# A coupled-map automaton on TensorE: ring products in pairs on two row tiles, and the convolution map of the same image beside it

## The chip, the core and the metric

The kernel runs on one NeuronCore of a Trainium2 chip. The metric is the device time of one execution in microseconds, the median of three runs. A profile is one further execution, recorded by the hardware profiler.

In the profile PE is TensorE's matmul side, PEld its weight loads, DVE VectorE, ACT ScalarE, POOL GpSimd and SP SyncE. POOL and SP issue the DMAs here, each in the order of its own queue. L393 means line 393 of the kernel before.

## The reference

The input has 32 images of 8 channels and 256 x 256 pixels. Four layers follow one another, each on a group-normalized input with its result added to the input. The change is in the first layer only:

```python
drive = x[:, :C_OUT]
grid = drive
for _ in range(STEPS):                       # 15 steps
    mapped = R * grid * (1.0 - grid)
    local = _conv(mapped, K_local, groups=C_OUT)      # 3x3, one kernel per channel
    physics = (1.0 - EPS) * mapped + EPS * local
    grid = (1.0 - BETA) * physics + BETA * drive
cml_out = jnp.clip(grid, 0.0001, 1.0 - 0.0001)
h = jax.nn.relu(_conv(x, Wp, bp))            # 3x3, 8 -> 128
nca_out = jax.nn.sigmoid(_conv(h, Wu, bu))   # 1x1, 128 -> 8
gin = jnp.concatenate([x, cml_out, nca_out], axis=1)
g = jax.nn.sigmoid(_conv(jax.nn.relu(_conv(gin, Wg1, bg1)), Wg2, bg2))   # 3x3, 24 -> 8, then 1x1
return g * cml_out + (1.0 - g) * nca_out
```

Below, the 15 steps are the automaton (`lattice` in the code), `h` and `nca_out` the map, and the last lines the gate. The remaining layers are a quantized 3x3 convolution, a 3x3 convolution and a 5x5 box filter; they run after the first layer has finished for all images, in a second part of the kernel that the change leaves alone.

## The kernel before

All data is fp32. An fp32 product appears in the trace as two matmul instructions, each with its weight load.

**The automaton.** Six of the eight channels (`CP = 6`) are computed on TensorE, the other two on VectorE. For TensorE the image is cut into patches of 16 rows by 8 columns: the 128 pixels of a patch lie on the 128 partitions, and the 512 patches of a channel on the free dimension. Neighbours within the patch come from one product with a 128 x 128 matrix (`patch_sb`, L391). Neighbours in the surrounding patches come from a second product that is added to it (`ring_sb`, L393). Its input, the tile `rings`, holds 80 rows, copies of the border rows of the state, shifted to the neighbouring patch: 16 for the left column, 16 for the right, and 24 each for the rows above and below (8 pixels times the patch itself and its two side neighbours). `spread` makes these copies with four SP DMAs (L259), each row with the data of three channels.

The channels are in two halves of three (`HALF`). For each half in a step the code issues three patch products, three ring products, three vector operations that add the drive out of PSUM (L402), and, after some other work, three squarings on ScalarE that write the next state (L419), and `spread`. PSUM has three buffers for these products. The two remaining channels are nine multiply-adds on VectorE (`tap`, L338), three beside the first half and six beside the second, then a clamp and the next state (L412, L413); `edges` copies the border rows of their strips with two SP DMAs (L263, L264).

**Map and gate.** `gated` is a generator of small pieces of work for PE, ACT, DVE and POOL. An image has eight chunks (`NCH`) of 512 columns; a chunk has four batches of four products `ph` (L633), each followed by a relu to `hh` (L638) and then by products with 32 output columns into `pn` (L610), four of which go to different column tiles. Six DMAs per batch bring the inputs `im` from `xn_d` (L505), a DRAM copy of the normalized image with borders. `close` takes the sigmoid of `pn` into `nh`, a tile in SBUF with room for four chunks, and issues small copies of its border rows (L480). The gate of a chunk begins five batches after the chunk. It loads the quarter image `xq` from `nr_d` and the automaton's result `cq` from `cr_d`, multiplies them and `nh` (L531, L539, L543), applies a second product (L548), mixes the results in seven vector operations (L561 to L568) and stores to `x1_d` (L569).

**The order** is written out by hand in one pass. Each `yield` of `lattice` and of `gated` gives a planned duration. The main loop at the end steps through `lattice(b)` and, after each yield, takes pieces of `gated` until their planned times have used up those of the automaton. `place` holds the chunk that the map has reached. Map and gate of image b-1 are taken beside the automaton of image b; beside image 0 there is nothing. `errands(b)` issues the loads, stores and statistics around an image one at a time, one per half step, on POOL and VectorE: the store of the normalized image to `xn_d` (L273), the load of the next image, the store to `nr_d` (L296), and to `xr_d` (L311).

Of the kernel before, what the change touches and what calls it, by code (L numbers as in the profile page):

```python
# [9 lines left out]
F32 = mybir.dt.float32  # L10
# [7 lines left out]
P = 128  # L18
C = 8
# [20 lines left out]
    (32, 8, (RB - 1) * PW, 1, -1 - SY, 3, SY),  # L40
    (56, 8, 0, 1, 1 - SY, 3, SY),
)
RING = 80
# [3 lines left out]
HALF = CP // 2  # L47
RQ = 4
BLOCK = 6.3
# [17 lines left out]
def kernel(  # L67
# [100 lines left out]
    with ExitStack() as es:  # L168
# [9 lines left out]
        ring_sb = const(wt, ring, [RING, CP, P], "ring_sb")  # L178
# [41 lines left out]
        nh = wt.tile([P, 8, WP], F32, name="nh")  # L220
        zero = wt.tile([C, WP], F32, name="zero")
        states = [wt.tile([P, HALF, SN], F32, name=f"state{i}") for i in range(2)]
        rings = [wt.tile([RING, HALF, SN], F32, name=f"rings{i}") for i in range(2)]
# [4 lines left out]
        for t in (*xbs, nh, zero, strip):  # L228
            nc.gpsimd.memset(t, 0.0)
        for t in (*states, *rings):  # L230
            nc.gpsimd.memset(t, 0.25)
# [5 lines left out]
        nr_d = [dram.tile([P, HB, WP], F32, name=f"nr_d{i}") for i in range(3)]  # L237

        cr_d = [dram.tile([P, HB, WP], F32, name=f"cr_d{i}") for i in range(3)]
        for t in xn_d:  # L240
            nc.sync.dma_start(
                window(t, 0, [[HP * WP, C], [(HP - 1) * WP, 2], [1, WP]]),
                nh[0:C, 0:2, :],
            )

        def inner(c):

            return states[c // HALF][:, c % HALF, AT : AT + TX * SY].rearrange("p (x y) -> p x y", y=SY)[:, :, 0:TY]

        def spread(half):  # L250

            long = (HALF - 1) * SN + RN
            state = states[half]
            row = state.ap[0][0]
            to = rings[half].rearrange("p c n -> p (c n)")
            for q, n, p, step, far, m, by in RINGS:
                at = p * row + AT + far
                dims = [[step * row, n]] + ([[by, m]] if m > 1 else []) + [[1, long]]
                nc.sync.dma_start(to[q : q + n * m, 0:long], window(state, at, dims))  # L259
# [6 lines left out]
        def errands(b):  # L266
# [3 lines left out]
            if b >= 0:  # L270
                xb = xbs[b % 2]
                for r in four:
                    nc.gpsimd.dma_start(  # L273
                        window(
                            xn_d[b % 3], (1 + r.start) * WP,
                            [[HP * WP, C], [RB * WP, HB], [1, 4 * WP]],
                        ),
                        xb[:, r, :].rearrange("p r w -> p (r w)"),
                    )
                    yield  # L280
# [47 lines left out]
        def lattice(b, ahead):  # L328
# [21 lines left out]
            )  # L350
            yield 5
            for t4 in range(TX // 4):
# [6 lines left out]
                if t4 == 0:  # L359
                    nc.vector.tensor_scalar(  # L360
                        xi, xi, st[:, 0:1], st[:, 1:2], ALU.subtract, ALU.mult
                    )
                if t4 == 4 and b > 0:
                    store(b - 1)
                if t4 == 1:
# [7 lines left out]
            for c in range(CP):  # L373
# [6 lines left out]
                if c % HALF == HALF - 1:  # L380
                    spread(c // HALF)
                yield 1.5
            yield 4
            for step in range(STEPS):
                for half in range(2):
                    mine = range(HALF * half, HALF * half + HALF)
# [5 lines left out]
                    for c in mine:  # L392
                        nc.tensor.matmul(  # L393
                            pss[c % HALF], ring_sb[:, c, :],
                            rings[half][:, c % HALF, 0 : TX * SY].rearrange(
# [4 lines left out]
                    for c in mine:  # L400
                        ps = pss[c % HALF]
                        nc.vector.scalar_tensor_tensor(ps, ps, FLOOR, dr[:, c], ALU.max, ALU.add)  # L402
                    if step == STEPS - 1:
                        for c in mine:
                            nc.vector.tensor_scalar(
                                dr[:, c], pss[c % HALF], 0.0001, 1.0 - 0.0001, ALU.max, ALU.min
# [636 lines left out]
```

## Time and profile before

| what | us |
|---|---|
| median of three runs | 16303.53 |
| lowest and highest of the runs | 16277.27 and 16305.33 |
| the profiled execution | 16318.33 |
| span of its profile, first to last instruction | 16316.6 |
| automaton of image 0 begins | 33.8 |
| automaton of image 1 and map of image 0 begin | 381.7 |
| last automaton ends | 13342.8 |
| last store of the first layer (L569) | 13594.8 |

The first layer is 83% of the span. The page has 42888 matmul instructions in it, twice the number of fp32 products. Times in the profile's answers count from the start of the span. The page's share of busy PE must be read with care, since a matmul's end is modelled and matmuls overlap; starts are better evidence than durations. For the DMAs of SP the page gives no time to landing.

### The profile page before, as it was taken

How to read it: one execution, taken by the hardware profiler on the slowest of the kernel's cores; microseconds unless marked ns; L12 is line 12 of the kernel's file. 1: busy time of each engine (PE TensorE's matmuls, PEld its weight loads, DVE VectorE, ACT ScalarE, POOL GpSimd, SP SyncE). 2: the span in 40 equal slices, each digit the busy share in tenths (PEclk: the TensorE clock that was granted, in tenths of full speed). 3: DMA queues.
4: the chain of work that ended last, by engine and by line, in shares of the span. 5: the costliest groups of instructions: out<-in, count | busy, mean ns of one | idle time of the engine just before them, and what ended most of it. 6: DMA issues, size and time to landing. Idle time of an engine off the chain costs nothing.

```text
span 16316.6 us, 141125 instructions
## 1 busy us (share of the span) xinstructions
PE 15452.2 (95%) x42888; PEld 6215.7 (38%) x42888; DVE 11705.9 (72%) x14652; ACT 5726.7 (35%) x8862; POOL 5598.2 (34%) x9491
## 2 busy tenths in 40 slices
PE   6999999999999999999999999999999997999999
PEld 2333333333333333333333333333333332333333
DVE  7777777777777777777777777777777764555554
ACT  2433444443434434443434444343444442111110
POOL 1333333333333333333333333333333342111111
PEclk7999999999999999999999999999999998999999
DMA  4766666666666666666666666666666664555554
GB/s 104 148 146 144 150 147 144 147 150 146 149 144 148 150 147 147 144 147 145 147 142 149 148 144 147 141 148 146 147 149 147 146 134 98 119 119 119 119 118 105
DMA packets 1057742, 2276.12 MB, mean 139 GB/s; under 512 B 419740, under 2 KB 623508, under 8 KB 1050724
## 3 DMA queue, kind: packets, MB, share of 16 engines
q0 software_dynamic: 704512, 1492.80, 40.6%
q1 hardware_dynamic: 352484, 774.29, 23.4%
q8 instruction: 356, 5.83, 0.2%
q14 instruction: 390, 3.19, 0.1%
HBM read 1078.04 MB, written 471.38 MB: 95 GB/s over the span
## 4 chain that ended last, share of the span: by engine, by line
PE 74%; DVE 13%; DMA 7%; ACT 3%; issue 2%; SPq 1%; POOL 0%; DVEq 0%; ACTq 0%; POOLq 0%
PE ph L633 17%; PE psc L391 14%; PE psc L393 13%; PE pg L531 9%; DVE acc L338 7%; PE psv L725 5%; PE pn L610 5%; PE psv L811 4%; DMA qb<-qh 3%; DMA rings<-state 2%; PE psv L729 2%; PE pq L548 1%; PE pg L543 1%; PE pg L539 1%; DVE psc L402 1%
## 5 line engine op out<-in xcount | busy, mean ns | idle before, releaser
L338 DVE SCALAR_TENSOR_TENSOR acc<-strip,taps_sb,acc 128x1024 f32<-128x1024 f32 x3840 | 4930.4, 1284 | 124.8 <-DMA strip<-strip 4.7
L505 POOL DMA_DIRECT2D im<-xn_d x6144 | 3458.3, 566 | 3250.0 <-PE ph L633 1434.7
L633 PE MATMUL ph<-im,wp_sb 72*128 72x512 f32 x8192 | 4091.7, 615 | 308.8 <-ACT hh L638 251.3
L638 ACT ACTIVATE hh<-ph,bp_sb 128x512 f32<-128x512 f32 x4096 | 2755.8, 690 | 4441.9 <-PE ph L633 4385.7
L402 DVE SCALAR_TENSOR_TENSOR psc<-psc,flat 128x512 f32<-128x512 f32 x2880 | 1921.4, 696 | 2813.0 <-PE psc L393 2797.2
L391 PE MATMUL psc<-state,patch_sb 128*128 128x512 f32 x5760 | 2812.0, 626 | 74.1 <-ACT state L419 63.3
L393 PE MATMUL psc<-rings,ring_sb 80*128 80x512 f32 x5760 | 2713.5, 607 | 129.8 <-DMA rings<-state 129.8
L633 PEld LDWEIGHTS ph<-im,wp_sb 72*128 72x128 f32 x8192 | 1489.5, 193 | 2425.4 <-issue 1587.8
L419 ACT ACTIVATE state<-psc,minus 128x512 f32<-128x512 f32 x2688 | 1690.2, 690 | 1818.8 <-DVE psc L402 1713.1
L391 PEld LDWEIGHTS psc<-state,patch_sb 128*128 128x128 f32 x5760 | 1114.5, 199 | 1696.2 <-issue 1375.7
L393 PEld LDWEIGHTS psc<-rings,ring_sb 80*128 80x128 f32 x5760 | 1114.7, 194 | 1576.8 <-issue 1545.7
L569 POOL DMA_DIRECT2D x_d<-xc x256 | 146.9, 574 | 3493.1 <-DVE xc L564 3416.6
L811 PE MATMUL psv<-xr,w_sb 128*128 128x512 f32 x2560 | 1162.9, 600 | 1.3 <-DVE xr L792 1.3
L610 PE MATMUL pn<-hh,wu_sb 128*32 128x512 f32 x8192 | 1133.9, 609 | 3.3 <-ACT hh L638 3.3
L776 POOL DMA_DIRECT2D x_d<-x x512 | 321.0, 643 | 1941.0 <-DVE x L770 1696.3
L725 PE MATMUL psv<-xh,w_sb 128*128 128x512 f32 x1536 | 753.0, 629 | 9.6 <-issue 9.6
L531 PE MATMUL pg<-xq,wg_sb 128*128 128x512 f32 x1536 | 749.3, 626 | 0.0
L754 ACT ACTIVATE x<-psv,b_sb,sc 128x512 f32<-128x512 f32 x256 | 199.3, 779 | 1466.2 <-PE psv L729 1465.8
L531 PE MATMUL pg<-cq,wg_sb 128*128 128x512 f32 x1536 | 713.7, 601 | 0.0
L811 PEld LDWEIGHTS psv<-xr,w_sb 128*128 128x128 f32 x2560 | 466.1, 189 | 610.8 <-issue 606.0
L338 DVE SCALAR_TENSOR_TENSOR acc<-strip,taps_sb,d 128x1024 f32<-128x1024 f32 x480 | 613.2, 1277 | 0.0
L831 DVE TENSOR_TENSOR y<-psv,y 128x512 f32<-128x512 f32 x256 | 177.1, 692 | 593.7 <-PE psv L811 593.7
(163 smaller groups left out, 12188.9 us busy)
## 6 DMA issues: line engine op xcount, KB each, us to landing
im<-xn_d POOLq DMA_DIRECT2D x6144, 96.6 KB, 6.6
rings<-state SPq DMA_DIRECT2D x1920, 159.5 KB
rings<-state SPq DMA_DIRECT2D x1920, 106.3 KB
strip<-strip SPq DMA_DIRECT2D x960, 126.0 KB
xn_d<-xb POOLq DMA_DIRECT2D x128, 516.0 KB, 7.7
nr_d<-xb POOLq DMA_DIRECT2D x128, 516.0 KB, 7.2
xq<-nr_d POOLq DMA_DIRECT2D x128, 516.0 KB, 5.1
cq<-cr_d POOLq DMA_DIRECT2D x128, 516.0 KB, 7.9
```

The source lines that it names most:

```text
L338: nc.vector.scalar_tensor_tensor(acc, strip[:, dy : dy + RQ, dx : dx + W], taps_sb[:, 3 * dy + dx : 3 * dy + dx + 1], d2 if dy == 1 and dx ...
L391: nc.tensor.matmul(pss[-1], patch_sb[:, c, :], inner(c), start=True, stop=False)
L393: nc.tensor.matmul(pss[c % HALF], ring_sb[:, c, :], rings[half][:, c % HALF, 0 : TX * SY].rearrange("p (x y) -> p x y", y=SY)[:, :, 0:TY], ...
L402: nc.vector.scalar_tensor_tensor(ps, ps, FLOOR, dr[:, c], ALU.max, ALU.add)
L419: nc.scalar.activation(inner(c), pss[c % HALF], AF.Square, bias=minus)
L505: nc.gpsimd.dma_start(im[24 * dy : 24 * dy + 24, k, 0:run], window(xn_d[b % 3], at, [[HP * WP, C], [1, 3], [1, run]]),)
L531: nc.tensor.matmul(o, wg1_sb[:, s, dx, :], src[:, :, dx : dx + W], start=s == dx == 0, stop=False,)
L610: nc.tensor.matmul(pn[32 * q : 32 * q + 32, :], wu_sb[:, i, :], hh, start=i == 0, stop=i == 3,)
L633: nc.tensor.matmul(ph.rearrange("p (k w) -> p k w", w=W), wp_sb, im[:, :, j * WP : j * WP + W], start=True, stop=True,)
L638: nc.scalar.activation(hh, ph, AF.Relu, bias=bp_sb)
L725: nc.tensor.matmul(o, w[:, dx, :], src[:, 2 * i : 2 * i + 2, dx : dx + W], start=dx == 0, stop=False,)
L811: nc.tensor.matmul(pss[k].rearrange("p (c w) -> p c w", w=W), w3_sb[:, dx, :], xr[:, k, mine, dx : dx + W], start=dx == 0, stop=stop,)
```

## The change

**Ring products in pairs.** The channels are taken in pairs (0, 3), (1, 4), (2, 5). The ring has 56 rows rather than 80: the rows above and below are split into 8 for the patch itself and 4 for the two corners (2 pixels times two side neighbours). One channel of the pair has its rows at partitions 0 to 55 (`LOW`), the other at 64 to 119 (`HIGH`) of the same tile, so that the two ring products use the upper and the lower half of the array and write different PSUM buffers. The state is kept in two sets, one with pairs 0 and 1, one with pair 2 (`SETS`). `spread(i)` copies a whole set: six DMAs for each side, twelve together, each row with two channels for set 0 and one for set 1.

**Order within a step.** Three pairs follow each other with 0.8 + 0.8 planned us between them and 8.6 + 0.8 after the third, the same 12.6 per step as the two halves had. `spread` follows the squares of pair 1 and pair 2, and `edges` the latter. The nine multiply-adds are spread 2, 2 and 5.

**Map beside the same image.** The store to `xn_d` moves from `errands` to the head of `lattice`, right after the normalization, which moves up too. `place[1]` is a limit: beside image 0 the map may reach chunk 7 of that image; beside image b it finishes chunk 7 of image b-1 first and then, once `store(b-1)` is issued, goes up to chunk 7 of image b.

**The map's result in DRAM.** The gate starts 33 batches after its chunk, instead of 5. So `nh` goes to DRAM (`nh_d`, three buffers) by one store per chunk, `keep_result`, and the gate loads it back like the other two inputs (`nq`), with its border rows. The copies of border rows from SBUF go.

```diff
-    (32, 8, (RB - 1) * PW, 1, -1 - SY, 3, SY),
-    (56, 8, 0, 1, 1 - SY, 3, SY),
+    (32, 8, (RB - 1) * PW, 1, -1, 1, 0),
+    (40, 8, 0, 1, 1, 1, 0),
+    (48, 2, (RB - 1) * PW, PW - 1, -1 - SY, 2, 2 * SY),
+    (52, 2, 0, PW - 1, 1 - SY, 2, 2 * SY),
 )
-RING = 80
+RING = 56
+LOW, HIGH = 0, 64
-HALF = CP // 2
+PAIRS = CP // 2
+SETS = ((0, 2), (2, 1))
-BLOCK = 6.3
+BLOCK = 12.6
...
-        def spread(half):
-
-            long = (HALF - 1) * SN + RN
-            state = states[half]
-            row = state.ap[0][0]
-            to = rings[half].rearrange("p c n -> p (c n)")
-            for q, n, p, step, far, m, by in RINGS:
-                at = p * row + AT + far
-                dims = [[step * row, n]] + ([[by, m]] if m > 1 else []) + [[1, long]]
-                nc.sync.dma_start(to[q : q + n * m, 0:long], window(state, at, dims))
+        def spread(i):
+
+            long = (SETS[i][1] - 1) * SN + RN
+            to = rings[i].rearrange("p c n -> p (c n)")
+            for state, base in zip(states[i], (LOW, HIGH)):
+                row = state.ap[0][0]
+                for q, n, p, step, far, m, by in RINGS:
+                    at = p * row + AT + far
+                    dims = [[step * row, n]] + ([[by, m]] if m > 1 else []) + [[1, long]]
+                    nc.sync.dma_start(
+                        to[base + q : base + q + n * m, 0:long], window(state, at, dims)
+                    )
...
+            nc.vector.tensor_scalar(xi, xi, st[:, 0:1], st[:, 1:2], ALU.subtract, ALU.mult)
+            for r in range(0, RB, 4):
+                nc.gpsimd.dma_start(
+                    window(
+                        xn_d[b % 3], (1 + r) * WP, [[HP * WP, C], [RB * WP, HB], [1, 4 * WP]]
+                    ),
+                    xb[:, r : r + 4, :].rearrange("p r w -> p (r w)"),
+                )
...
                 if t4 == 4 and b > 0:
                     store(b - 1)
+                    place[1] = NCH * (b + 1) - 1 if b + 1 < B else NCH * B
...
-            for c in range(CP):
+            for c in (0, 3, 1, 4, 2, 5):
...
-                if c % HALF == HALF - 1:
-                    spread(c // HALF)
+                if c >= PAIRS + 1:
+                    spread(c - PAIRS - 1)
...
+            taps_of = (((1, 0), (1, 1)), ((1, 2), (0, 0)), ((0, 1), (0, 2), (2, 0), (2, 1), (2, 2)))
             for step in range(STEPS):
-                for half in range(2):
-                    mine = range(HALF * half, HALF * half + HALF)
+                for j in range(PAIRS):
+                    i = j // 2
+                    mine = (j, PAIRS + j)
...
-                    for c in mine:
+                    for ps, base in zip(pss, (LOW, HIGH)):
                         nc.tensor.matmul(
-                            pss[c % HALF], ring_sb[:, c, :],
-                            rings[half][:, c % HALF, 0 : TX * SY].rearrange(
+                            ps, ring_sb[base : base + RING, j, :],
+                            rings[i][base : base + RING, j - SETS[i][0], 0 : TX * SY].rearrange(
                                 "p (x y) -> p x y", y=SY
                             )[:, :, 0:TY],
                             start=False, stop=True,
                         )
...
-                    yield 1.7
+                    yield 0.8
                     if step < STEPS - 1:
-                        for c in mine:
-                            nc.scalar.activation(inner(c), pss[c % HALF], AF.Square, bias=minus)
-                        spread(half)
-                        if half == 1:
+                        for c, ps in zip(mine, pss):
+                            nc.scalar.activation(inner(c), ps, AF.Square, bias=minus)
+                        if j == SETS[i][0] + SETS[i][1] - 1:
+                            spread(i)
+                        if end:
                             edges()
-                    next(ahead, None)
-                    yield BLOCK - 1.7
+                    if j != 1:
+                        next(ahead, None)
+                    yield BLOCK - 4.0 if end else 0.8
...
-                    for name, t in (("xq", nr_d), ("cq", cr_d)):
+                    for name, t in (("xq", nr_d), ("cq", cr_d), ("nq", nh_d)):
                         quarter[name] = qp.tile([P, 4, WP], F32, name=name)
                         nc.gpsimd.dma_start(quarter[name], t[b % 3][:, k0 : k0 + 4, :])
...
+            def keep_result():
+
+                n = done.pop()
+                b, r2 = divmod(n, NCH)
+                nc.gpsimd.dma_start(nh_d[b % 3][:, 2 * r2 : 2 * r2 + 2, :], nhs[n % 2])
...
-                due.setdefault(batch + 5, []).append(gate(n, quarter))
+                due.setdefault(batch + 4 * NCH + 1, []).append(gate(n, quarter))
...
                 ahead = errands(b)
+                place[1] = NCH * b if b > 0 else NCH - 1
                 for gap in lattice(b, ahead):
-                    if b > 0:
-                        left += gap
-                        while left > 0 and place[0] < b * NCH:
-                            left -= next(rest)
-                        left = min(left, 0.0)
+                    left += gap
+                    while left > 0 and place[0] < place[1]:
+                        left -= next(rest)
+                    left = min(left, 0.0)
```

## The prediction

> **What bounds the kernel now.** I read the page's busy shares first, then one row per stage, then the chain of waits inside the long stage, then what TensorE waited for there.
>
> ```profile
> PE 15452.2 (95%) x42888; PEld 6215.7 (38%) x42888; DVE 11705.9 (72%) x14652; ACT 5726.7 (35%) x8862; POOL 5598.2 (34%) x9491
> ```
>
> ```profile
> 34.00:382.00 348.00, 220.61 (x432) 93.36 (x433) 279.94 (x301) 69.35 (x106) 26.10 (x41) 0.75 0.44 92
> 382.00:13343.00 12961.00, 12511.86 (x35218) 4997.64 (x35218) 9833.16 (x11436) 5201.45 (x8143) 4976.20 (x8566) 0.97 0.68 146
> 13343.00:13603.00 260.00, 246.28 (x762) 89.25 (x760) 61.46 (x108) 112.58 (x163) 150.07 (x252) 0.98 0.50 121
> ```
>
> The columns are stretch, length, busy PE, PEld, DVE, ACT, POOL, clock, DMA share, GB/s. Image 0's automaton runs alone for 348 us. Then 31 periods hold the automaton of image b beside map and gate of b-1: 12961/31 = 418.1 us each, PE 97% busy. After the last automaton the last map and gates run alone, 252 us to the last x1 store at 13594.8. The later layers take the rest and are not touched.
>
> A busy PE can still be slow to feed, so the chain inside one period decides:
>
> ```profile
> 5107.73 2.77 PE psc L391 x6
> 5110.50 2.58 PE psc L393 x6
> 5113.08 1.72 PE ph L633 x4
> 5114.80 0.98 PE pg L539 x4
> 5115.78 1.06 PE pg L543 x2
> ```
>
> For 80 us around these lines the chain never leaves PE. One fp32 product is two matmul instructions of 0.43 us (2.58/6). What PE did wait for, over the 31 periods:
>
> ```profile
> PE ph L633 <- ACT hh L638: 251.3, 122, 4.9
> PE psc L393 <- DMA rings<-state: 100.9, 33, 6.1
> PE ph L633 <- DVE xb L431: 57.1, 30, 1.9
> ```
>
> Together 13 us of each 418. So a PE pass removed is worth nearly its whole time, until a wait replaces it. DVE has 317 us of work per period (9833/31), the next engine, with 100 us to spare.
>
> [...] The trace has only column tiles; [...] the two L539 products start 7 ns apart and four instructions take 0.98 us, not 1.72. [...] 0.98 is 0.12 over two passes, and the next product takes 1.06, 0.20 over its 0.86. [...]
>
> **Ring products.** Before: 6 products per step, 12 passes. After: 3 pairs, each two products of 56 rows at partitions 0 and 64. Nearest row for a pair is L539: 0.98 + 0.20 = 1.18 us. A row tile loads 128 weight columns where L539 loads 32 (L393's load is 194 ns, L539's 108), so add 0.09: 1.27 against 4 x 0.43 = 1.72. Saved: 0.45 x 45 pairs = 20.2 us per image. If the two did not overlap, a pair would cost 1.72 + 0.41 and 18 us would be lost; the column tiles speak against it.
>
> **SP's queue.** Before, a step issues 8 ring copies and 2 strip copies. After, it issues 12 for the set of two channels per side, 12 for the other and 2 strips.
>
> ```profile
> 5116.49 2.74 SPq L259 DMA_DIRECT2D rings<-state  x4
> 5123.69 0.83 SPq L263 DMA_DIRECT2D strip<-strip  x1
> 5124.56 0.80 SPq L264 DMA_DIRECT2D strip<-strip  x1
> ```
>
> Issues start 0.60 to 0.64 us apart (16 rows), about 0.71 for the corner copies (taken from L800, also two-dimensional on its source). A set costs 8 x 0.61 + 4 x 0.71 = 7.7 us instead of 2.8, SP's work per step 17 us instead of 7.3. It still fits a step of 22 us, but the delay grows. I took the landings from the trace's record of semaphore increments. Today a half's four copies need 11.0 us on average from first issue to last landing (10.8 median, 12.6 upper quartile, 8.6 when the automaton is alone); a 16-row copy takes 3.0 us alone and 5.6 beside the map. They use eight semaphores in turn, so the ninth of twelve also waits for the first to land. After, the last of twelve starts 7.0 us after the first; with 5.6 for landing that is 12.6, with the 8.7 that today's last copy takes, 15.7. Rows are shorter (4.5 KB and 2.2 KB against 6.8), which favours the low end[...].
>
> What is available: after pair 1's ring product come about 3.6 us until its squares are written (DVE 0.7 twice, ACT, an interleaved relu; 3.9 is typical for SP's start today), while PE does pair 2 (1.72 + 1.3) and the map's 0.8 + 0.8 + 0.8 + 8.6 units of planned work (a unit is close to a us), then pair 0's patches (1.72). That is 17 - 3.6 = 13.2 us. Today it is 16 to 17.5. So need and supply meet. I take 0.3 us of wait per step, 4.5 us per image; bounds 0 and 1.5 us (22 per image).
>
> **First ring data of an image.** Today PE waits up to 6.1 us there, once per image. The square order 0,3,1,4,2,5 releases the first set one channel later (2 us) and its issue is 4.9 us longer, against rows a third shorter: +4, bounds 2 to 8.
>
> **PSUM buffers.** Three buffers now serve pairs, so the second patch of pair 1 needs the square of pair 0 (3.0 us after its last pass: 0.7 + 0.7 + a relu + 0.7), and PE has 1.6 planned units plus one patch in between: 3.2. No slack, where three channels per half had about 4 us. The two weight lists put less than one map product there in few of 15 steps, about 0.8 us each. A gate's seven vector operations (some 4.9 us) mostly fall in the long gap; there DVE needs 8.5 us for five taps, clamp and next state plus 4.9, about 2 us over what the gap covers, five times an image. Part meets the ring wait of the same step. I take +5, bounds 2 to 12.
>
> **Start of an image.** The map now reads xn_d from the same image. The second 2.4 us normalization and four stores (0.63 us issue, 7.6 landing) stand on POOL ahead of the input loads of the next chunk; one chunk, 28 units, lies between. Behind the blocked POOL queue stand those loads and a gate's xc; they have some 28 us. +2, bounds 0 to 5.
>
> **nh through DRAM.** 256 stores, 128 loads of 516 KB and 256 halo loads replace 576 halo copies: 64 more POOL issues in 13.4 ms, at 0.57 us each 37 us on an engine 38% busy, and they are issued a whole image ahead of use. Nothing on the path; uncovered it would be a few us per gate.
>
> **Ends.** Map 0 runs beside automaton 0: I take 355 us instead of 348, DVE being the bound there. The tail holds one map chunk (20), eight gates of 9.8 us of PE (2.58 + 2.58 + 1.72 + 0.98 + 1.06 + 0.86) with about 1.5 us of ACT waits each (90), and the closing vector work (10): 120 instead of 252. Together -125; as the last gates may wait for loads I take -115, bounds -85 and -140.
>
> **Sum.** Per period -20.2 + 4.5 + 4 + 5 + 2 = -4.7; 31 x -4.7 = -146; with the ends -261. The profiled execution took 16318.3 us (span 16316.6), so 16057. The median of the runs shown is 15 us lower: 16040.
>
> **Rivals.**
> - *The saving is kept nearly whole* (0.22): ring data lands in about 12 us, waits at their low bounds: -20.2 + 4 = -16 per period, -500 and -115: 15690. For it: shorter rows, 13 us of waits today. Against: 24 issues in a row on one queue.
> - *The ring copies set the step* (0.32): 14.4 us from first issue to landing, 1.2 us per step. Per period -20.2 + 18 + 11 = +8.8; +273 - 115: 16460, slower. It decides from 0.86 us per step on (12.9 per image: -20.2 + 11 + 12.9 = +3.7, which is 115/31). For it: today's upper quartile of 12.6 with a third of the issues; against: row length.
> - *The row tiles run one after the other* (0.04): +18 + 15 per period, about 17200.
>
> **How the numbers follow.** The forecast case (0.42) spans 15900 to 16300 and is the likeliest. Its upper end touches no change: a measurement of this kernel tells about 0.2% (33 us) from nothing. From its 0.42, 0.37 lies below that, 0.05 within, none clearly above; the kept-whole case adds 0.22 to faster; the two slow ones give 0.36, of which 0.01 lies within 0.2%. Faster 0.59, same 0.06, slower 0.35. For 8 in 10 I leave out the lowest tenth and the highest: 15680 to 16530.
>
> **What would show it.** Ring instructions starting in twos a few ns apart, a pair at 1.2 to 1.35 us; if not, the tiles don't overlap. The period at 413 us; PE's wait for rings near 9 us per image (today 3.3), and for ACT behind the patches about 5. The stretch before 382 nearly unchanged, the tail near 120. The forecast is wrong if SP's twelve copies take over 14 us to land, if patches wait for squares more than 12 us per image, or if the map's loads stall at an image's start.

## The result and the profile after

| | before | after |
|---|---|---|
| median of four runs each, same chip, us | 16297.88 | 16565.92 |
| lowest and highest | 16277.27 to 16305.33 | 16538.26 to 16582.17 |
| profiled execution | 16318.33 | 16569.87 |
| automaton of image 0 | 347.9 | 391.6 |
| a period, mean of 30 | 418.2 | 428.7 |
| from the last automaton's end to the last x1 store, measured as last automaton start to store, less one period | 249.4 | 125.4 |

The ratio is 1.0167, 95% interval 1.0154 to 1.0180: slower, where faster was forecast. The three stages account for it: +44 for image 0, 31 x 10.56 = +327 for the periods, -124 for the tail, together +247 of the 251.5 us between the two profiled executions.

The page of the kernel after, busy shares:

```profile
PE 15211.9 (92%) x42888; PEld 5507.1 (33%) x42888; DVE 11612.4 (70%) x14652; ACT 5792.1 (35%) x8864; POOL 5570.7 (34%) x9558
```

Its stages, with the columns of the table of stages before:

```profile
32.00:424.00 392.00, 316.71 (x879) 107.01 (x883) 276.69 (x302) 145.14 (x228) 123.30 (x212) 0.92 0.47 115
424.00:13286.00 12862.00, 11912.24 (x34092) 4183.23 (x34085) 9439.15 (x11095) 5106.13 (x7883) 4800.36 (x8366) 0.94 0.59 141
13286.00:13850.00 564.00, 514.66 (x1445) 183.50 (x1443) 368.70 (x451) 198.10 (x303) 205.28 (x345) 0.94 0.52 130
```

PE has less work and is idle more: in the middle stage it is 93% busy (11912 of 12862) where it was 97%, and its granted clock is 0.94 where it was 0.97. Both count. Now what PE waited for over 30 periods:

```profile
PE psc L406 <- DMA rings<-state: 417.5, 119, 11.5
PE psc L404 <- ACT state L431: 317.4, 271, 4.6
PE ps L109 <- DVE mv L106: 99.7, 29, 3.8
PE psc L404 <- DVE flat L417: 42.6, 30, 1.5
PE psc L406 <- issue: 25.3, 7, 7.2
PE ph L645 <- ACT gt L561: 18.3, 29, 1.0
PE ph L645 <- ACT hh L650: 11.9, 27, 1.4
```

L404 is the patch product, L406 the ring product, L431 the square. Per period the wait for ring copies went from 3.3 us to 13.9, the patches' wait for squares (a PSUM buffer held until the square has read it) from none to 10.6, a wait of the next image's statistics from none to 3.3; the map's wait for its relus fell from 8.2 to 0.4. One step of one image, TensorE's timeline:

```profile
5033.01 1.88 PE L404 MATMUL psc<-state,patch_sb 128*128 128x512 f32 x4
5034.82 1.12 PE L406 MATMUL psc<-rings,ring_sb 56*128 56x512 f32 x2
5039.22 1.12 PE L406 MATMUL psc<-rings,ring_sb 56*128 56x512 f32 x2 [3.28 <-DMA rings<-state]
5040.27 0.38 PE L329 MATMUL ps<-st,pick_sb 128*128 128x2 f32 x2
...
5044.96 1.13 PE L406 MATMUL psc<-rings,ring_sb 56*128 56x512 f32 x4
5046.02 1.98 PE L645 MATMUL ph<-im,wp_sb 72*128 72x512 f32 x4
```

and SyncE's timeline in the same stretch:

```profile
5024.01 19.45 SPq L272 DMA_DIRECT2D rings<-state  x19
5043.56 0.86 SPq L278 DMA_DIRECT2D strip<-strip  x1
```

The pair at 5044.96 is whole: four instructions, the next product 1.06 us later. The pair at 5034.82 is torn. The side at partitions 0 to 55 starts; the side from 64 on, whose six copies come second in SyncE's queue, starts 4.4 us later. SyncE works through 19 ring copies in these 19.45 us, so those of the set of pair 2 go on until after it. A torn pair also loses the overlap. Of the 1350 pairs of the 30 periods 127 are torn, 4.2 a period, 98 of them pair 0 and 29 pair 2; 9.9 of the 13.9 us of rings' wait lie inside them. While the first side runs by itself, 1.12 us here, the list counts no wait; but the second side then takes 1.05 us, as long as a whole pair, so that time is lost too. At 4.2 pairs of 1.1 us I estimate some 4 us a period that the late copies cost beyond the wait that is listed.

### The profile page after: what moved, and what is told of

It reads as the page before. It is cut to its first block, busy times and chain, and to the rows that moved or that the text cites. A ratio compares the mean times of both kernels' runs of the same rounds, so it can differ in the third digit from the quotient of the medians.

```text
span 16568.1 us, 158674 instructions
## 1 busy us (share of the span) xinstructions
PE 15211.9 (92%) x42888; PEld 5507.1 (33%) x42888; DVE 11612.4 (70%) x14652; ACT 5792.1 (35%) x8864; POOL 5570.7 (34%) x9558
## 5 line engine op out<-in xcount | busy, mean ns | idle before, releaser
L645 PE MATMUL ph<-im,wp_sb 72*128 72x512 f32 x8192 | 4346.4, 646 | 69.5 <-DMA im<-xn_d 34.6
L650 ACT ACTIVATE hh<-ph,bp_sb 128x512 f32<-128x512 f32 x4096 | 2792.0, 687 | 4194.4 <-PE ph L645 4129.7
L414 DVE SCALAR_TENSOR_TENSOR psc<-psc,flat 128x512 f32<-128x512 f32 x2880 | 1872.6, 693 | 3096.2 <-PE psc L406 3083.9
L404 PE MATMUL psc<-state,patch_sb 128*128 128x512 f32 x5760 | 2982.4, 631 | 380.5 <-ACT state L431 335.3
L431 ACT ACTIVATE state<-psc,minus 128x512 f32<-128x512 f32 x2688 | 1714.7, 687 | 2713.1 <-DVE psc L414 2385.0
L406 PE MATMUL psc<-rings,ring_sb 56*128 56x512 f32 x5760 | 1882.9, 669 | 481.1 <-DMA rings<-state 455.4
L404 PEld LDWEIGHTS psc<-state,patch_sb 128*128 128x128 f32 x5760 | 1062.3, 198 | 2143.9 <-issue 1143.3
L406 PEld LDWEIGHTS psc<-rings,ring_sb 56*128 56x128 f32 x5760 | 497.4, 191 | 1732.8 <-issue 1160.3
```

The costliest lines, as they stand in the source:

```text
L404: nc.tensor.matmul(pss[-1], patch_sb[:, c, :], inner(c), start=True, stop=False)
L406: nc.tensor.matmul(ps, ring_sb[base : base + RING, j, :], rings[i][base : base + RING, j - SETS[i][0], 0 : TX * SY].rearrange("p (x y) -> ...
L431: nc.scalar.activation(inner(c), ps, AF.Square, bias=minus)
L645: nc.tensor.matmul(ph.rearrange("p (k w) -> p k w", w=W), wp_sb, im[:, :, j * WP : j * WP + W], start=True, stop=True,)
L650: nc.scalar.activation(hh, ph, AF.Relu, bias=bp_sb)
```

## The experiments

Three theories. **A:** the ring copies come too late, since a set has twelve of them on one queue. **B:** three PSUM buffers for pairs have a price of their own. **C:** the row tiles cost more than they save. Each run was compared with the kernel before on its own chip (medians there 16290 to 16321 us); ratios are to it. "Half clock" is the time per period in which the trace's record of the granted clock shows half speed: 27.7 us before, 52.0 after. Adding up the gaps between matmul starts, TensorE is idle for about 4 of the 27.7 and 11 of the 52.0; only the rest is work at half speed.

**The pairs alone** (`pairs_only`): the kernel before with pairs, rings, sets and step order of the change; the map stays one image behind, with its result in SBUF. Of the change this takes back:

```diff
-                due.setdefault(batch + 4 * NCH + 1, []).append(gate(n, quarter))
+                due.setdefault(batch + 5, []).append(gate(n, quarter))
...
-                        while left > 0 and place[0] < place[1]:
+                        while left > 0 and place[0] < b * NCH:
```

> The kernel before with the pairs alone: paired ring products on two row tiles, 56-row rings, the new step order and ring copies; map and gate stay one image behind and nh stays in SBUF. Theory A (late ring copies: twelve SP copies in a row land 13 us after the first, PE waits, and the waits pull the clock down) and theory B (three PSUM buffers serve pairs, so a patch product waits for a square) both expect the period of after, about 428 us, with the ends of before (348 and 252 us): 16298 + 31 x 10.5 = 16620 us. Theory D (the map beside its own image lengthens the period) expects a period of about 415 and 16200 us.

Measured 16520.87, ratio 1.0127 (1.0106 to 1.0148). Image 0 took 334.2, a period 424.4, the tail 244.1. Waits per period: squares 11.9, rings 11.3; half clock 41.1. So the pairs carry +6.2 of the +10.6 us a period; the expectation's theory D, that the map beside its own image is what lengthens it, would have left about 415. The rest of the change adds 4.3, makes image 0 57 us longer and the tail 119 shorter: 31 x 4.3 + 57 - 119 = +71, no gain.

**No row tiles** (`tiles_off`), on the kernel after: each ring product reads all 128 rows, with zero weights on the other channel's.

```diff
-                    for ps, base in zip(pss, (LOW, HIGH)):
+                    for c, ps in zip(mine, pss):
...
-                            ps, ring_sb[base : base + RING, j, :],
-                            rings[i][base : base + RING, j - SETS[i][0], 0 : TX * SY].rearrange(
+                            ps, ring_sb[:, c, :],
+                            rings[i][:, j - SETS[i][0], 0 : TX * SY].rearrange(
```

> The changed kernel with each ring product over all 128 rows, the other side's weights zero: the same copies, order and results, but no row tiles, 20 us more PE work per period. A expects most of it to be absorbed, since each added PE pass gives the copies more time: PE's wait for rings falls from 13.9 to about 6 us per period, period 433 to 440, 16700 to 16940 us, half-clock time falls somewhat, from 52 to about 40 us. Theory C (the row tiles and their mode changes themselves lower the clock) expects the half-clock time back at 28 us with ring waits near 12. If nothing is absorbed the period is 449 and the time 17190 us.

Measured 16709.94, ratio 1.0242 (1.0226 to 1.0258), period 432.4. Its stretch of the profile beside that of the kernel after, 5000 to 10000 us (first tiles_off, then after):

```profile
5000.00:10000.00 5000.00, 4656.79 (x13208) 1840.32 (x13207) 3670.92 (x4285) 1989.55 (x3052) 1865.20 (x3235) 0.97 0.59 140
```

```profile
5000.00:10000.00 5000.00, 4633.27 (x13294) 1628.47 (x13292) 3669.44 (x4308) 1989.17 (x3071) 1876.98 (x3272) 0.94 0.60 142
```

C falls in its plain form: row tiles still gain 3.7 us a period. But they should gain some 20, and the clock column says where much of that goes: without them half clock is 28.8 us a period, with them 52.0. That is what C's expectation had said of the clock (28). A's had been that the rings' wait falls to about 6 and half clock to about 40; the wait rose to 17.3. No pair can be torn here, since each product needs the rows of both sides; so the wait stands whole in the list, and the 17.3 are to be compared with the 13.9 and the 4 or so that torn pairs hide.

**Half of the copies** (`no_high`), on the kernel after: the copies to partitions from 64 on are left out, so channels 3 to 5 get stale ring rows.

```diff
-            for state, base in zip(states[i], (LOW, HIGH)):
+            for state, base in zip(states[i], (LOW,)):
```

> The changed kernel without the ring copies of the HIGH side (12 instead of 24 per step); channels 3 to 5 then compute with a ring that stays 0.25. A expects PE's wait for rings under 3 us per period, half-clock time near 30, period about 406, 15860 us. B expects the waits for squares to stay at 10 us or grow, half clock to stay near 50, period about 417, 16220 us. C expects half clock at 52 whatever the waits.

**Short rows** (`short_rows`): all copies are issued, but each row is cut to 64 values; the rest of the ring rows is stale.

> The changed kernel with all 24 ring copies issued but each row cut to its first 64 values; the rest of the ring stays 0.25, so the automaton computes with a wrong ring. If the copies are late by what their bytes take on the DMA engines, the wait for rings falls under 3 us per period and the time is as in no_high, about 15860 us. If they are late by issue and by the turn of eight semaphores, the wait stays above 8 us and the time above 16350 us.

Measured 15881.44, ratio 0.9740 (0.9718 to 0.9761), and 15951.44, ratio 0.9773 (0.9755 to 0.9791). The periods are 406.1 and 408.9. Waits of no_high, and its stretch of 5000 us:

```profile
PE psc L404 <- ACT state L431: 332.8, 298, 3.8
PE psc L406 <- DMA rings<-state: 137.8, 26, 9.1
```

```profile
5000.00:10000.00 5000.00, 4713.30 (x13957) 1661.20 (x13956) 3874.34 (x4574) 2087.43 (x3229) 1954.38 (x3409) 0.97 0.58 134
```

The rings' wait fell by 9.3 us a period, the squares' wait did not move (11.1), and the period fell by 22.7. Two things make up most of the other 13.4 us. Half clock fell from 52.0 to 27.5, also with row tiles, so that C's "52 whatever the waits" is refuted; with TensorE's idle time in it taken off (11 us and 4), half of the rest is about 9 us. And no pair is torn any more, which gives some 4.

So the copies come too late. By the trace's semaphore increments a set's twelve copies with two channels each take 12.6 us on average within the steps (13.1 with the first set of each image), the six of no_high 8.8. A single copy lands no sooner in no_high (5.0 us in the median, 3.9 after), but the set's last issue comes 3.4 us after its first rather than 7.9. That points to the issue; no_high moves half of the bytes as well, so it is no proof.

The short rows don't separate bytes from issue. Their rings' wait is 5.2 us a period, under the 8 of the one expectation and over the 3 of the other. But 64 values belong to pair 0 alone, so these copies need not wait for pair 1's squares: the first is issued 4.7 us before the first of those squares ends (median), where in the kernel after it follows that square. Counted from the first issue, a set is not faster than before the cut (13.4 us on average). What the run shows is that the steps don't wait for copies that begin earlier and carry fewer bytes: all but one of its 28 torn pairs are in the first step of an image.

**A fourth PSUM buffer** (`psc4`, on the kernel after) is taken from the pool of the map's products; `pairs_psc4` is the same on the pairs alone.

```diff
-        ps_c = es.enter_context(tc.tile_pool(name="ps_c", bufs=3, space=PSUM))
+        ps_c = es.enter_context(tc.tile_pool(name="ps_c", bufs=4, space=PSUM))
...
-        psum = es.enter_context(tc.tile_pool(name="ps_a", bufs=3, space=PSUM))
+        psum = es.enter_context(tc.tile_pool(name="ps_a", bufs=2, space=PSUM))
```

> The kernel after with one change: the PSUM pool of the patch and ring products has four buffers instead of three, and the pool of the transposes and of the map's products two instead of three. Theory A (the ring copies are late): the PSUM wait only hides part of the ring wait. The patches' wait for squares falls from 10.6 us a period to under 3, but the rings' wait rises from 13.9 towards 20 and the period stays between 426 and 430 us. Theory B (three buffers for pairs is a cost of its own): the squares' wait of 10.6 and the 3.3 for the DVE drive add go, the rings' wait rises by less than 4, and the period falls by 8 to 15 us, 16100 to 16320 in all. Under both the map's wait for the relu may grow by 2 to 8 us, since its products have a buffer less.

> The kernel before with the ring products in pairs alone (map one image behind, its result in SBUF), and four PSUM buffers for the patch and ring products as above. Theory A: ring copies keep the period near that of the pairs alone, 422 to 426 us, 16430 to 16560 in all. Theory B: the period falls to 410 to 416, and with 334 us for image 0 and a tail of 244 the time is 16080 to 16260, below the kernel before.

Measured 16872.98, ratio 1.0348 (1.0326 to 1.0371), and 16793.85, ratio 1.0298 (1.0279 to 1.0318): both slower than any theory said. The waits of psc4:

```profile
PE psc L406 <- DMA rings<-state: 338.9, 153, 6.2
PE ph L645 <- ACT hh L650: 262.3, 312, 3.1
```

The squares' wait is gone, and the map with two banks waits 8.7 us a period for relus in its place, in 312 short waits; half clock rose to 67.0. The bank was needed where it was, so these two runs do not decide B.

**Half of the copies on GpSimd's queue** (`high_on_pool`) **and more map work between the pairs** (`wide_gaps`), on the kernel after:

```diff
-                    nc.sync.dma_start(
+                    (nc.sync if base == LOW else nc.gpsimd).dma_start(
```

```diff
-                    yield 0.8
+                    yield 1.3
...
-                    yield BLOCK - 4.0 if end else 0.8
+                    yield BLOCK - 6.5 if end else 1.3
```

> The kernel after with one change: the six copies of each set to partitions 64 and up are issued by GpSimd's queue, the six others stay with SyncE's. Nothing is left out. Theory A, in the form that one queue's issue and its turns of semaphores make the copies late: two queues issue six each, the twelve land some 3 to 4 us earlier, the rings' wait falls from 13.9 us a period to about 5 and the period by 10 to 18 us, to 411 to 419, 16020 to 16270 in all. Theory A in the form that the DMA engines are the limit (the bytes that wait in them): no gain, 428 us or more a period. A third way: GpSimd's queue holds the copies behind the map's loads and stores that wait[...], so the copies come later than before: 435 us or more a period.

> The kernel after with one change: the planned durations between the pairs of a step are 1.3 instead of 0.8, so that more of the map's products stand between the pairs, and 2.5 us fewer after the third. Theory B: the square of pair 0 has 2 us more until the second patch of pair 1 asks for its buffer, so the squares' wait falls from 10.6 us a period to under 4; the ring copies of the first set have as much time as before (what stands after pair 2 is less, what stands before it is more), so the rings' wait stays at 12 to 16 and the period falls by 4 to 8 us. Theory A: the time that the squares' wait takes is given back at the rings, and the period stays at 426 to 430.

Measured 16918.18, ratio 1.0372 (1.0355 to 1.0389), period 439.9, with the rings' wait at 24.3 us a period: the third way of its expectation, in its result. The trace shows the queue: GpSimd's issue takes 0.52 us a copy, no more than SyncE's (0.65 us in the median in the kernel after), and in the median step the last of its six copies of the first set lands 6.0 us after pair 1's second square. But in one step of twenty GpSimd issues the first of them only 14.9 us after that square or later, and the last lands over 21 us after it. And 16676.23, ratio 1.0226 (1.0204 to 1.0249), period 431.0: the squares' wait stayed (10.2), in fewer and longer waits, and the rings' wait rose to 15.6. I had taken the first set's room to be unchanged; but more work between pair 0 and pair 1 makes the squares of pair 1 later, and the room smaller: from the first issue to pair 0's ring product it is 12.8 us in the median step, and 14.2 in the kernel after.

**The sums in SBUF** (`sums`), on the kernel after: DVE's addition of the drive writes to an SBUF tile, and the square reads that. A PSUM buffer is free after DVE, and no bank is taken from anybody.

```diff
-                        nc.vector.scalar_tensor_tensor(ps, ps, FLOOR, dr[:, c], ALU.max, ALU.add)
+                        v = hp.tile([P, 512], F32, name="v", bufs=2)
+                        vs.append(v.rearrange("p (x y) -> p x y", y=TY))
+                        nc.vector.scalar_tensor_tensor(vs[-1], ps, FLOOR, dr[:, c], ALU.max, ALU.add)
...
-                        for c, ps in zip(mine, pss):
+                        for c, ps in zip(mine, vs):
                             nc.scalar.activation(inner(c), ps, AF.Square, bias=minus)
```

> The kernel after with one change: the DVE operation that adds the drive writes to an SBUF tile (two buffers) instead of back into PSUM, and the squares read that tile, so that a PSUM buffer of the patch and ring products comes free with the DVE operation and not with the square. No bank is taken from anybody. Theory B (the three buffers have a price of their own): the squares' wait of 10.6 us a period goes, about a third of it comes back as a wait for DVE, half-clock time falls from 52 towards 40, and the period falls by 8 to 14 us to 415 to 421. Theory A (the ring copies bind, the squares' wait only lies in front of theirs): the rings' wait rises from 13.9 to about 20 and the period falls by 4 us at most.

Measured 16422.58, ratio 1.0081 (1.0066 to 1.0096), period 423.7. The waits:

```profile
PE psc L406 <- DMA rings<-state: 436.0, 153, 11.2
PE psc L404 <- DVE v L416: 197.0, 150, 3.4
```

The patches wait 6.6 us for DVE where they waited 10.6 for ACT; the rings' wait is nearly the same (14.5). The period fell by 5.1, between A's 4 and B's 8: B holds for about that much.

**Corners on ScalarE's queue** (`corners_act`, and with the sums in SBUF on both forms, `sums_act` and `pairs_sums_act`):

```diff
-                    nc.sync.dma_start(
+                    (nc.scalar if m > 1 else nc.sync).dma_start(
```

> The kernel after with one change: the four corner copies of each set (two per side) are issued by ScalarE's queue, the other eight by SyncE's. Nothing is left out. Theory A: a set's issue on SyncE takes 5 us instead of 7.5 and the ninth copy's wait for the first landing goes; the last landing comes about 3 us sooner, the rings' wait falls from 13.9 us a period to 4 to 8 and the period by 6 to 14. The rival: ScalarE gives 0.6 to 0.7 us to each of eight corner issues in a step, 5 us, in front of the map's relus; the products then wait for relus by 10 us a period or more, and the period stays at 425 or rises.

> Both edits above together on the kernel after. If theories A and B each hold for their part: period 402 to 414 us, 15750 to 16120 in all, below the kernel before. If only A holds, as for the corners alone, 414 to 422. If ScalarE's issues hold up the relus, 420 and above.

> The same two edits on the kernel before with the ring products in pairs alone (period 424.4, image 0 in 334, tail 244). If A and B each hold for their part: period 400 to 411 us, and with the longer tail 15800 to 16140 in all. If ScalarE's issues hold up the relus, 418 and above, 16300 or more.

Measured 17370.51, 17420.48 and 17277.47, ratios 1.0668 (1.0645 to 1.0691), 1.0692 (1.0675 to 1.0708) and 1.0599 (1.0579 to 1.0619). Waits of corners_act:

```profile
PE ph L645 <- ACT hh L650: 637.2, 200, 8.2
...
PE psc L406 <- DMA rings<-state: 50.1, 25, 4.6
```

The rings' wait went to 1.7 us a period, as A has it, and the relus behind ScalarE's copies cost 21.2, with others like them; half clock is 81.7. ScalarE spends 80 us a period on issuing these copies, 0.63 us each in the median, and is idle for another 21 right ahead of them, until they may be issued. A wait was removed and a larger one made.

**Room for the first set** (`tight`, and `sums_tight` with the sums in SBUF), on the kernel after: no map work between pair 0 and pair 1; it stands behind pair 2. Every copy stays on SyncE.

```diff
-                    yield 0.8
+                    yield 0.8 if j > 0 else 0
...
-                    yield BLOCK - 4.0 if end else 0.8
+                    yield BLOCK - 2.4 if end else 0.8 * j
```

> The kernel with the sums in SBUF (above), and the map work of 1.6 planned us between pair 0 and pair 1 moved behind pair 2; nothing else. Theory A (the copies of the first set take 13 us and have 13.2): the squares of pair 1 and with them the copies of the first set come about 1.6 us earlier against the next step's pair 0, so 14.8 us are there; the rings' wait falls from 14.5 us a period to 5 to 9, and the period from 423.7 to 414 to 419, 16120 to 16290 in all. Theory B: pair 1's second patch follows pair 0 more closely, its wait for the DVE sum rises from 6.6 to 10 or more, and the gain is under 3 us a period.

> The kernel after with one change: the map work of 1.6 planned us between pair 0 and pair 1 moved behind pair 2, the sums still in PSUM. If the room of the first set alone decides (theory A), the period falls by about 10 us as it did with the sums in SBUF, to 417 to 420, 16190 to 16310. If the buffers hold their part by themselves (theory B beside A), pair 1's second patch now asks for its buffer about 1.6 us earlier: the squares' wait rises from 10.6 us a period to 15 or more, and the period stays at 424 or above.

Measured, tight: 16295.92, ratio 1.0003 (0.9994 to 1.0012), period 418.6, no difference from the kernel before. Sums_tight: 16124.14, ratio **0.9891** (0.9875 to 0.9907), period 413.2: faster than both kernels. Waits of sums_tight, and its stretch of 5000 us:

```profile
PE psc L406 <- DMA rings<-state: 322.2, 103, 12.2
PE psc L404 <- DVE v L416: 202.4, 253, 3.7
PE ph L647 <- ACT hh L652: 58.3, 58, 1.6
```

```profile
5000.00:10000.00 5000.00, 4729.51 (x13780) 1659.24 (x13779) 3788.63 (x4492) 2100.01 (x3185) 1943.60 (x3374) 0.96 0.62 146
```

The two edits add up: -5.1 (sums), -10.1 (tight), -15.6 (both) us a period. In tight the squares' wait rose less than B had it (12.0), and the rings' wait fell to 10.1. Of tight's gain the larger part is the clock, half clock 52.0 to 32.9; in sums_tight it is 37.0.

**All map work behind the pairs** (`sums_tight2`), and both orders on the pairs alone:

> As the run before, with the map work between pair 1 and pair 2 moved behind pair 2 as well. Theory A: nothing more for the first set, whose room counts from pair 1's squares to the next pair 0, so the rings' wait and the period are within 2 us of the run before. Theory B: two places where a patch waits for a DVE sum, 6 us a period more than the run before. A loss at both would say that the pairs need work of the map between them.

> The kernel before with the pairs alone, the sums in SBUF and the map work between pair 0 and pair 1 moved behind pair 2. Theory A: rings' wait from 11.3 us a period to 4 to 7, period from 424.4 to 409 to 415, image 0 about 330, tail 244: 15990 to 16180 in all, below the kernel before. Theory B: above 417 a period, 16230 or more.

> As the run before, with the map work between pair 1 and pair 2 moved behind pair 2 as well. Theory A: within 2 us a period of the run before. Theory B: 4 to 8 us a period more.

Measured 16403.51 (ratio 1.0062, 1.0047 to 1.0077), 16195.17 (0.9939, 0.9925 to 0.9954) and 16235.49 (0.9962, 0.9948 to 0.9976). After the change the second gap is needed: without it the period is 422.5, the rings' wait 14.6 and the wait for DVE sums 9.3. On the pairs alone the two orders give 416.0 and 415.7. So "within 2 us" held there and not in the other; why the two forms differ was not followed up. The first order is just outside A's range there (409 to 415, and a rings' wait of 9.7 where 4 to 7 was expected). The two orders reach the same period with different parts: the waits for DVE sums are 6.3 and 10.1 us, half clock is 42.7 and 27.1. So more waiting does not always mean more half clock.

## Why the prediction was wrong

Its own steps, per period where nothing else is said, the kernel after against the kernel before. The clock is priced at half of the time at half clock, since in the trace of the kernel after two map instructions that follow each other start 0.43 us apart at full clock and 0.85 inside half clock. Half of the 24.3 us of added half clock is 12; with TensorE's idle time in it taken off, (52.0 - 11) - (27.7 - 4), half is about 9:

| step | forecast | measured |
|---|---|---|
| ring products | -20.2 | -20.7 |
| ring waits: steps and first data | +8.5 | +10.6 |
| torn pairs, first side alone | none | +4, estimated |
| PSUM buffers | +5 | +12.0 |
| statistics of the next image, image start | +2 | +3.3 |
| map's waits for relus and xb | none | -9.6 |
| half clock | none | +9, estimated |
| sum | -4.7 | +8.6, of +10.6 measured |
| image 0 | +7 | +44 |
| tail | -132 | -124 |

**Right.** Tiles do run together: a pair starts 7 ns apart and takes 1.26 us where 1.27 was worked out, 45 x (1.72 - 1.26) = 20.7 for pairs that are whole. The copies' need was right: 12.6 us on average within the steps, where 12.6 to 15.7 were named. The room came out near by luck: the terms named for it add up to 15.7 and not to 17, which leaves 12.1 and not 13.2; from first issue to pair 0's ring the median step has 14.2. The tail came out at 125 for 120. Of the three signs named for a wrong forecast only one came, and only in image 0: a stall of the map's loads at an image's start. The copies stayed under 14 us on average and the patches' wait for squares under 12.

**The ring waits were nearly right, and the rival's size was not.** "I take 0.3 us of wait per step": in the trace's waits the ring instructions of an image's first step wait 9.2 us a period (before: 3.2) and those of the fourteen later steps 5.6, 0.4 each (before: none). These count 0.8 us beyond the 13.9, which the list puts down to "issue". So the rival with 1.2 us a step did not come about by its sum, though the time it gave, 16460, is nearer. The reason that a mean need of 12.6 against a room of 13 to 14 waits at all is the spread: within the steps 36% of the sets take over 13.2. The mean of the excess over 13.2 is 1.1 us, over 14.8 it is 0.6.

**The step that failed: the sum counts each wait at its own length.** "So a PE pass removed is worth nearly its whole time, until a wait replaces it" leaves out what comes with the wait. The named waits were forecast at +15.5 and came to +16.3, right in total by luck: the buffers were 7 over and the map's waits 9.6 under. The sum has no term for the clock, where half clock nearly doubled and costs about 9 us, and none for pairs that are torn, another 4: 13 of the 15.3 us between -4.7 and +10.6. With half of the copies gone half clock is back at 27.5, no pair is torn, and the period is 22.7 shorter for 9.3 us of rings' wait. So the second half of the copies costs more than twice what its waits show. That late copies bring the loss is shown; what sets the amount of half clock is not. It is 28.8 with no row tiles and 32.9 with more room for the first set, but 67.0 with a fourth buffer and 81.7 with the corners on ScalarE, where waits ahead of the map's products took the place of others.

**Mis-sized: the PSUM buffers.** "+5, bounds 2 to 12" was 10.6 for squares and 1.4 for the last step's clip, at the upper bound. I had the place right, the second patch of pair 1, and took "part meets the ring wait of the same step" for relief; no_high shows that it doesn't: 9.3 us of rings' wait went and the squares' wait stayed. Sums show that 5.1 us a period can be had back there.

**Mis-sized: the ends.** Image 0 was to take 355 us and took 391.6. One wait is as long as most of that, of a map product for its inputs from `xn_d`:

```profile
PE ph L645 <- DMA im<-xn_d: 26.5, 1, 26.5
```

In PE's order the automaton's products stand behind it. Beside it image 0 has 24.5 us of waits for ring copies. "I take -115" was -80, and with the 4.3 us a period that the own-image part adds, the part loses. In the trace's waits the first step's ring wait is 5.7 on the pairs alone and 9.2 after: the first set of an image lands 39.6 us after the image's start there and 43.9 after (36.4 before). The squares' wait is 1.3 less, and half clock rose as well, from 41.1 to 52.0; so the 4.3 do not lie in the first step alone. That the four stores to `xn_d`, which now stand right ahead of them, are what delays them fits, and was not tried.

**Not foreseen on the good side:** the map's wait for relus, 8.2 us before, is 0.4 after. It was part of the 13 us that I had read as given.

**What stays open:** why row tiles and waits together bring so much more half clock than longer waits without row tiles. How much of the copies' lateness is issue and how much bytes: no run changes one alone. And how much of the 10.1 us of tight is the room of the copies (rings' wait -3.8) and how much the mere place of the map's products (half clock -19).

## What to carry to other kernels

Where a transfer's need is about as long as its room, take the mean of the excess over the room, not the excess of the mean, and look at the clock column before pricing a wait: here 9.3 us of waits were worth 22.7 us, because half clock and torn pairs went with them. Two products that are to run side by side need their data at the same time: in the torn pair shown above the late side alone took as long (1.05 us) as a whole pair (1.06). Moving the corner copies to ScalarE's queue put their issue, 80 us a period, and another 21 of waits in front of that engine's own work; moving the work around the copy, and freeing a buffer one engine earlier, cost nothing here and turned 1.7% slower into 1.1% faster. And an overlap of stages that shortens the tail once is to be set against what it adds in every period.

## What the runs showed of the hardware

- Two fp32 products of 56 rows at partitions 0 and 64 (four instructions of 512 columns, in the kernel after) take 1.06 us to the next product's start and 1.26 with entry and exit; two of 128 rows after one another take 1.72 (tiles_off).
- In the trace's record of the granted clock, half clock comes in stretches of 3.41 us and multiples of it: of the 152 in the 30 periods of the kernel after, 19 last 3.41 us, 47 twice and 54 four times as long (5.1 stretches a period after, 3.9 before). The longest gap between two matmul starts in the 8 us before a stretch is 3.6 us in the median after and 3.1 before; in sums_tight, half of the stretches begin with none above 2.6 us.
- The same twelve ring copies (two channels a row, in the kernel after) take 7.5 to 11.8 us from first to last issue and have landed after 9.8 to 18.0 us (5th to 95th percentile, within the steps) beside the map's loads.
- Eight DMA issues a step moved to ScalarE's queue (corners_act), on an engine 35% busy in the kernel after, lengthened the period by 24 us, although the wait that they were to shorten went from 13.9 to 1.7 us.
